# Three buffers in place of two for the tile of delta, in the preparation between the scan loops

## The chip, the cores and the metric

The kernel runs on one core of one Trainium2 chip. The metric is the device time of one execution in microseconds (us); lower is better. It is given as the median of several runs. One execution was also taken by the hardware profiler, and the profile and its trace come from that one.

## What is computed

A stack of four layers works on images x of shape (4, 64, 64, 96). The first two are selective-scan layers (the change lies in them), the last two are an attention without softmax and a feed-forward net. A scan layer, cut to what matters here:

```python
xz = einsum('bhwc,ec->bhwe', groupnorm(x), in_proj_w)      # E = 192, then z beside it
xc = silu(depthwise_conv3x3(xx) + conv_b)
xs = stack([x_hw, x_wh, x_hw[..., ::-1], x_wh[..., ::-1]]) # four directions, L = 4096 steps each
x_dbl = einsum('bkdl,kcd->bkcl', xs, x_proj_weight)        # dts (6), B (16), C (16)
delta = softplus(einsum('bkrl,kdr->bkdl', dts, dt_projs_weight) + dt_projs_bias)
# scan: h = exp(delta * A) * h + delta * B * u ;  y = sum_n h * C
y = layernorm(y_0 + flip(y_2) + back(y_1) + back(flip(y_3))) * silu(z)
out = x + einsum('bhwe,ce->bhwc', y, out_proj_w)
```

What the scan needs of each direction is delta itself and the product of delta and u. Delta has to reach the scan in nearly full precision, although it passes through a bf16 matmul there; so it is cut into three bf16 parts that add up to it.

## The kernel before

The batch is worked in two pairs of images, and with two scan layers that makes four phases. Each phase has a preparation, a scan loop, and a finish. `run` (L699) goes through the phases: it builds the preparation of phase p side by side with the finish of phase p-1, then the scan loop of phase p. So on the time axis a scan loop is followed by a gap in which the next preparation and the last finish share the engines, and then by the next scan loop. Before the first loop there is a preparation alone. After the last loop come a finish alone and the two token layers. The text calls the stretches between the scan loops, and the one before the first, "gaps".

Inside a scan loop the order of instructions on every engine is written out by hand (`manual_schedule`, L490). In the gaps it is not: there a scheduler orders each engine's instructions at build time, from the dependencies, the buffers and its own estimate of times. Each engine then takes its instructions strictly in that order at run time, and waits at the first one that is not ready. The DMAs are issued by the SP engine, from its own queue of instructions, also in order.

A preparation (`prepare`, L151) reads x, takes the statistics of the group norm, and runs `convolve` (L231) for each of the two images: a matmul (L251), the copy of its result into a padded tile (L254), nine taps of the convolution on VectorE (L268; the first, L266, on ScalarE), silu (L271), and a scaled copy that is stored for the finish (L276, L282). The second image's convolution runs between the calls of `steps` for the first image.

`steps` (L284) is where the change lies. There are 32 calls in a preparation: two images, eight chunks of 512 steps, two of the four directions; each call also does the opposite direction, so it makes a pair of tiles. In order:

- the matmul to dts, B and C (L291), and two copies into `xd`, forward and mirrored (L294, L295);
- the store of B and C (L303), and for both directions the matmul to delta's argument, into a PSUM tile `d` with two buffers (L308);
- then, for each of the two directions, a tile `dl` of delta (96 x 2 x 512 float32): softplus on ScalarE (L316); the first bf16 part, a cast on ScalarE (L317); the product with u on VectorE (L318); delta less its first part, written over delta on VectorE (L319); two stores of the product (L321); the second part, a cast on GpSimd (L322); the third part on VectorE (L323); the store of the three parts (L324).

`dl`, `parts`, `du_sb` and `xd` come from the pool `steps`, made with two buffers for each name (L168). A tile that is asked for when all its buffers are in use has to wait until the last reader of the oldest is done. For `dl` that is L323. For `parts` and `du_sb` it is the landing of their stores.

The finish (`finish`, L546) loads the scan's results (`yk`, L581, and `ud_f`, L571), adds the four directions through matmuls (L594, L603, copied out by L610), normalises (L633 to L648), multiplies with silu of z (L660, L663, L667), transposes (L674, L681) and projects (L685, L687), and stores the new x (L693).

Of the kernel before, what the change touches and what calls it, by code (L numbers as in the profile page):

```python
# [9 lines left out]
F32 = mybir.dt.float32  # L10
# [12 lines left out]
C = 96  # L23
# [6 lines left out]
TC = 512  # L30
# [25 lines left out]
def scan_view(t, k, c):  # L56


    part, half = t.ap[0], t.ap[1]
    if k == 0:  # L60
        off, steps = TC * c, (HW, 1)
    elif k == 1:
        off, steps = ROWS * c, (1, HW)
    elif k == 2:
        off, steps = L - 1 - TC * c, (-HW, -1)
    else:
        off, steps = L - 1 - ROWS * c, (-1, -HW)
    return bass.AP(t.tensor, t.offset + off, [part, half, [steps[0], ROWS], [steps[1], HW]])


def view(t, off, *dims):

    return bass.AP(t.tensor, t.offset + off, [t.ap[0]] + [list(d) for d in dims])


def rows(t):

    if len(t.shape) == 2:
        return t.rearrange("p (r w) -> p r w", w=HW)
    return t.rearrange("p h (r w) -> p h r w", w=HW)  # L80
# [50 lines left out]
class Scans:  # L131
# [152 lines left out]
    def steps(self, ph, sp, xc, xp, dt_w, i, k, c):  # L284


        nc, cst = self.nc, self.cst
        u = scan_view(xc, k, c)
        ps = self.bank()
        for h in range(2):  # L290
            nc.tensor.matmul(rows(ps[:XD2]), xp[:, k, h], u[:, h], start=h == 0, stop=h == 1)  # L291
        xd = sp.tile([XD2, TC], F32, name="xd")

        nc.scalar.activation(xd[:XD], ps[:XD], AF.Identity, bias=cst.one_row[:XD])  # L294
        nc.scalar.activation(  # L295
            xd[64:], view(ps[64:XD2], TC - 1, (-1, TC)), AF.Identity, bias=cst.one_row[64:]
        )
        yield
        both = []
        for back in range(2):  # L300
            at = 64 * back
            g, cc = 2 * (k + 2 * back) + i, NC - 1 - c if back else c
            nc.sync.dma_start(ph.bc[cc][:, g], xd[at : at + 2 * NS])  # L303
            both.append((g, cc, scan_view(xc, k + 2 * back, cc), self.p_d.tile([C, 2, TC], F32, name="d")))
        for m in range(2):
            for back, (_, _, _, ps) in enumerate(both):
                part = slice(64 * back + 2 * NS, 64 * back + XD)
                nc.tensor.matmul(  # L308
                    ps[:, m], dt_w[part, k, m * C : (m + 1) * C], xd[part], start=True, stop=True
                )  # L310
        yield
        for g, cc, u, ps in both:
            delta = sp.tile([C, 2, TC], F32, name="dl")
            parts = sp.tile([C, NP16, 2, TC], BF16, name="parts")
            du = sp.tile([C, 2, TC], F32, name="du_sb")
            nc.scalar.activation(delta, ps, AF.Softplus)  # L316
            nc.scalar.copy(parts[:, 0], delta)  # L317
            nc.vector.tensor_tensor(rows(du), rows(delta), u, ALU.mult)  # L318
            nc.vector.tensor_tensor(delta, delta, parts[:, 0], ALU.subtract)  # L319
            for copy in range(2):  # L320
                nc.sync.dma_start(ph.du[cc][copy, g, :E].rearrange("(h e) t -> e h t", h=2), du)  # L321
            nc.gpsimd.tensor_copy(parts[:, 1], delta)  # L322
            nc.vector.tensor_tensor(parts[:, 2], delta, parts[:, 1], ALU.subtract)  # L323
            nc.sync.dma_start(  # L324
                ph.delta[cc][g].rearrange("n (h q) t -> q (n h) t", h=2),
                parts.rearrange("q n h t -> q (n h) t"),
            )
            yield
# [660 lines left out]
```

## Time and profile before

| | |
|---|---|
| median of 3 runs | 11985.35 us (11978.79 to 12007.12) |
| the profiled execution's own time | 11973.68 us |
| its span in the trace | 11971.9 us |
| granted TensorE clock, mean over the span | 0.826 of full |
| busy: TensorE matmul | 8659.6 us (72%) |
| busy: VectorE | 10052.3 us (84%) |
| busy: ScalarE | 7321.2 us (61%) |
| busy: GpSimd | 7465.3 us (62%) |

Times are in us, lengths of one instruction in nanoseconds where a row says "mean ns". PE is TensorE, PEld its weight load, DVE VectorE, ACT ScalarE, POOL GpSimd, and SP the engine whose queue issues the DMAs. In the page each engine has a row of 40 slices of the span; a digit is the busy share of a slice in tenths, and PEclk is the clock that TensorE was granted, in tenths of full speed. A row of the timeline gives start, length, engine, line, operation, and what is written and read; in brackets stands how long the engine was idle before it and what ended the wait. A row of waits gives who waited for what, the total, how often, and the longest.

### The profile page before, as it was taken

The page shows a single profiled execution, that of the slowest core. Times are in us where ns is not written, and L with a number is a line of the kernel's source. Part 1 is how long each engine was busy: PE and PEld are TensorE (multiplying, and loading weights), DVE is VectorE, ACT ScalarE, POOL GpSimd, SP SyncE. Part 2 cuts the span into 40 slices and gives each one's busy share as a digit, 9 for nine tenths or more (in the row PEclk, how much of TensorE's full clock was granted, in tenths as well). Part 3 has the DMA queues.
Part 4 walks back from the last instruction along what each step waited for, and adds up shares of the span by engine and source line. Part 5 has one row for each costly group of instructions (what it writes and reads, how often), then busy time and mean ns, then how long its engine had stood idle before and what let it go on. Part 6 is the DMA issues. An engine that isn't in the chain of part 4 may idle for free.

```text
span 11971.9 us, 337755 instructions
## 1 busy us (share of the span) xinstructions
PE 8659.6 (72%) x144960; PEld 4597.6 (38%) x144960; DVE 10052.3 (84%) x10351; ACT 7321.2 (61%) x12109; POOL 7465.3 (62%) x2316
## 2 busy tenths in 40 slices
PE   3567777765767777765777777766677777777777
PEld 1124444442334444442334444433234444444333
DVE  6679999987769999987769999986769999993667
ACT  4556666655556666655556666654557666662556
POOL 0169999960149999970149999970139999990000
PEclk8579999986679989886679999986668999998887
DMA  3677777764677777765677777764677777763110
GB/s 98 185 244 254 255 252 252 252 206 138 197 231 255 254 256 257 257 216 143 193 226 256 258 257 252 258 219 136 199 221 258 255 254 250 254 232 125 18 21 11
DMA packets 952267, 2501.23 MB, mean 209 GB/s; under 512 B 324494, under 2 KB 607220, under 8 KB 819316
## 3 DMA queue, kind: packets, MB, share of 16 engines
q1 hardware_dynamic: 950772, 2479.63, 62.8%
q8 instruction: 1142, 18.71, 0.7%
q14 instruction: 353, 2.89, 0.1%
HBM read 1965.42 MB, written 513.80 MB: 207 GB/s over the span
## 4 chain that ended last, share of the span: by engine, by line
DMA 56%; PE 12%; DVE 11%; SPq 10%; ACT 5%; issue 4%; POOL 2%; POOLq 0%; DVEq 0%; ACTq 0%
DMA h<-du 52%; SPq L399 9%; DVE xc L268 4%; PE f L594 2%; POOL parts L322 2%; PE d L308 1%; PE c L291 1%; DVE parts L323 1%; DVE dl L319 1%; DVE du_sb L318 1%; DMA yk<-y 1%; PE c L251 1%; PE f L603 1%; PE f L674 1%; PE f L660 1%
## 5 line engine op out<-in xcount | busy, mean ns | idle before, releaser
L409 POOL TENSOR_TENSOR h<-h,b 128x1536 f32<-128x1536 f32 x2048 | 7021.1, 3461 | 533.5 <-DMA h<-du 191.9
L426 DVE TENSOR_TENSOR_SCAN h<-a,carry,h 128x512 f32<-128x512 f32 x5376 | 6345.7, 1259 | 174.6 <-POOL h L409 171.9
L419 ACT ACTIVATE a<-a,a_col 128x512 f32<-128x512 f32 x6144 | 4031.0, 664 | 1856.7 <-PE a L415 1830.9
L444 PEld LDWEIGHTS y<-h,cw 128*32 128x32 f32 x131072 | 2786.7, 128 | 3501.2 <-issue 1310.9
L444 PE MATMUL y<-h,cw 128*32 128x48 f32 x131072 | 3660.1, 266 | 527.3 <-DVE h L426 211.6
L415 PE MATMUL a<-dlt,rep 72*128 72x512 bf16 x6144 | 2526.8, 422 | 1302.3 <-DVE h L426 1212.9
L322 POOL CAST parts<-dl 96x1024 bf16<-96x1024 f32 x256 | 416.1, 1630 | 2793.0 <-DVE dl L319 2587.0
L456 ACT COPY d<-y 128x384 f32<-128x384 f32 x2048 | 979.8, 478 | 475.0 <-PE y L444 429.8
L426 DVE TENSOR_TENSOR_SCAN h<-a,h 128x512 f32<-128x512 f32 x768 | 868.3, 1200 | 165.5 <-ACT a L419 142.6
L415 PEld LDWEIGHTS <-rep 72*128 72x128 bf16 x6144 | 487.2, 98 | 829.0 <-issue 587.8
L308 PE MATMUL d<-xd,dt_w 7*96 7x512 f32 x1024 | 631.7, 905 | 237.5 <-ACT dl L316 149.6
L268 DVE SCALAR_TENSOR_TENSOR xc<-xp,conv_w,xc 96x512 f32<-96x512 f32 x1024 | 713.8, 756 | 54.8 <-ACT xc L266 38.9
L826 POOL MEMSET tn<- 1x4096 f32 x8 | 27.8, 3507 | 862.3 <-PE pa L846 515.1
L316 ACT ACTIVATE dl<-d 96x1024 f32<-96x1024 f32 x256 | 258.4, 1018 | 449.5 <-DVE parts L323 429.1
L318 DVE TENSOR_TENSOR du_sb<-dl,xc 96x1024 f32<-96x1024 f32 x256 | 416.2, 1633 | 116.7 <-ACT dl L316 73.0
L291 PE MATMUL c<-xc,x_proj 96*103 96x512 f32 x512 | 452.3, 1024 | 82.1 <-ACT xc L271 42.7
L594 PE MATMUL f<-yk,perm 128*128 128x384 f32 x1024 | 429.6, 564 | 95.4 <-DMA yk<-y 72.8
L251 PE MATMUL c<-rawi,in_w 96*96 96x512 f32 x256 | 206.0, 915 | 397.0 <-DVE rawi L247 312.1
L319 DVE TENSOR_TENSOR dl<-dl,parts 96x1024 f32<-96x1024 f32 x256 | 309.6, 1217 | 210.8 <-ACT parts L317 209.3
L323 DVE TENSOR_TENSOR parts<-dl,parts 96x1024 bf16<-96x1024 f32 x256 | 329.1, 1292 | 160.4 <-POOL parts L322 158.0
L308 PEld LDWEIGHTS d<-xd,dt_w 7*96 7x96 f32 x1024 | 171.8, 222 | 642.9 <-ACT dl L316 229.7
L361 ACT ACTIVATE cw<-c,gmask 128x256 f32<-128x256 f32 x512 | 286.0, 570 | 116.4 <-DMA dlt<-delta 58.1
(116 smaller groups left out, 5802.0 us busy)
## 6 DMA issues: line engine op xcount, KB each, us to landing
h<-du SPq DMA_DIRECT2D x1024, 768.0 KB
h<-du SPq DMA_DIRECT2D x2048, 384.0 KB
du<-du_sb SPq DMA_DIRECT2D x512, 384.0 KB
delta<-parts SPq DMA_DIRECT2D x256, 576.0 KB
dlt<-delta SPq DMA_DIRECT2D x512, 288.0 KB
y<-d SPq DMA_DIRECT2D x2048, 48.0 KB
yk<-y SPq DMA_DIRECT2D x256, 384.0 KB
ud<-xu SPq DMA_DIRECT2D x128, 192.0 KB
```

The costliest lines, as they stand in the source:

```text
L268: nc.vector.scalar_tensor_tensor(rows(acc), src, w, rows(acc), ALU.mult, ALU.add)
L291: nc.tensor.matmul(rows(ps[:XD2]), xp[:, k, h], u[:, h], start=h == 0, stop=h == 1)
L308: nc.tensor.matmul(ps[:, m], dt_w[part, k, m * C : (m + 1) * C], xd[part], start=True, stop=True)
L322: nc.gpsimd.tensor_copy(parts[:, 1], delta)
L399: self.nc.sync.dma_start(u.h[32 * first : 32 * (first + quarters), e : e + n].rearrange("p e t -> p (e t)"), source.rearrange("a g e t -> ...
L409: self.nc.gpsimd.tensor_tensor(h, h, b, ALU.mult)
L415: self.nc.tensor.matmul(u.a[n], self.cst.rep[:, h], u.dl[:, e], start=True, stop=True)
L419: self.nc.scalar.activation(u.a[n], u.a[n], AF.Exp, scale=u.ph.a_col[:, at : at + 1])
L426: self.nc.vector.tensor_tensor_scan(u.h[:, n], u.a.pop(n), u.h[:, n], 0.0 if u.c == 0 else u.ph.carry[:, at : at + 1], ALU.mult, ALU.add,)
L444: self.nc.tensor.matmul(view(u.y[32 * j : 32 * j + 32], l2 * EB, (8 * EB, 4), (1, EB)), u.ph.cw[u.c][:, l1, 8 * j + l2], view(u.h, 64 * l1 ...
L456: self.nc.scalar.copy(u.d[:, :, :, l1], u.y[:, : 32 * EB].rearrange("p (t h x) -> p t h x", t=4, h=2))
L594: nc.tensor.matmul(ps[:, : 4 * C].rearrange("p (w v e) -> p w v e", w=4, v=nv), cst.perm[:, k], view(t, off, (sw if k < 2 else -sw, 4), (1 ...
```

## The change

The tile of delta in `steps` gets three buffers of its own. The other tiles of the pool keep two. The operations are the same; the order on the engines is again the scheduler's.

```diff
         for g, cc, u, ps in both:
-            delta = sp.tile([C, 2, TC], F32, name="dl")
+            delta = sp.tile([C, 2, TC], F32, name="dl", bufs=3)
             parts = sp.tile([C, NP16, 2, TC], BF16, name="parts")
             du = sp.tile([C, 2, TC], F32, name="du_sb")
             nc.scalar.activation(delta, ps, AF.Softplus)
```

## The prediction

> **What bounds the kernel now.** I read the page first: the slices, then the chain that ended last. In the slices the 99999 stretches of DVE are the four scan loops; between them lie the stretches that the change touches. The chain's largest part, 52%, is the scan loops' load h<-du, which the change doesn't reach.
>
> ```profile
> span 11971.9 us, 337755 instructions
> DVE  6679999987769999987769999986769999993667
> PEclk8579999986679989886679999986668999998887
> ```
>
> By the first and last scan (L426) in the trace the loops run from 701 to 2599, 3437 to 5322, 6161 to 8035 and 8898 to 10769 us, so the gaps before them last 701, 838, 839 and 863 us. The first holds a preparation alone, the other three a preparation beside the finish of the phase before.
>
> Second, the windows of two kinds of gap (us, then busy time and count of PE, PEld, DVE, ACT, POOL, then clock and DMA). The reader is to see that in the first gap's end no engine but PE is near full, and that PE runs at half its clock; in a later gap's end PE is the fullest too.
>
> ```profile
> 550.00:600.00 50.00, 43.33 (x48) 11.27 (x47) 31.31 (x24) 21.01 (x24) 12.25 (x8) 0.50 0.77 224
> 3150.00:3250.00 100.00, 86.29 (x220) 39.88 (x220) 59.43 (x86) 52.58 (x64) 14.19 (x11) 0.67 0.73 214
> ```
>
> Third, the timeline of one pair of tiles in the first gap's end (A and B: the two directions of one call of steps; start, length).
>
> ```profile
> 544.43 1.22 DVE L323 TENSOR_TENSOR parts<-dl,parts 96x1024 bf16<-96x1024 f32 x1 [0.94 <-POOL parts L322]
> ...
> 545.75 1.02 ACT L316 ACTIVATE dl<-d 96x1024 f32<-96x1024 f32 x1 [5.32 <-DVE parts L323]
> ...
> 546.67 1.03 ACT L317 CAST parts<-dl 96x1024 bf16<-96x1024 f32 x1
> ...
> 547.73 1.22 DVE L319 TENSOR_TENSOR dl<-dl,parts 96x1024 f32<-96x1024 f32 x1 [2.08 <-ACT parts L317]
> ...
> 549.07 1.04 POOL L322 CAST parts<-dl 96x1024 bf16<-96x1024 f32 x1 [4.68 <-DVE dl L319]
> ...
> 550.14 1.22 DVE L323 TENSOR_TENSOR parts<-dl,parts 96x1024 bf16<-96x1024 f32 x1 [1.19 <-POOL parts L322]
> ...
> 551.29 1.22 DVE L318 TENSOR_TENSOR du_sb<-dl,xc 96x1024 f32<-96x1024 f32 x1
> ...
> 551.46 1.02 ACT L316 ACTIVATE dl<-d 96x1024 f32<-96x1024 f32 x1 [2.47 <-DVE parts L323]
> ...
> 552.50 1.04 ACT L317 CAST parts<-dl 96x1024 bf16<-96x1024 f32 x1
> ...
> 553.58 1.22 DVE L319 TENSOR_TENSOR dl<-dl,parts 96x1024 f32<-96x1024 f32 x1 [1.08 <-ACT parts L317]
> ...
> 556.87 1.22 DVE L323 TENSOR_TENSOR parts<-dl,parts 96x1024 bf16<-96x1024 f32 x1 [0.93 <-POOL parts L322]
> ```
>
> ACT takes its instructions in their order, and that order has the softplus L316 of a later tile ahead of the cast L317 of the tile before it. So L317, which needs nothing of L316, stands behind its wait for a free delta buffer: L323 ends, L316, L317, L319, L322, L323, one ring for every tile. A pair takes 12.44 us here; where u is read with the other stride L318 takes 1.9 us and the pair 13.1. The mean is 12.78, over 14 pairs from 513 to 692 us.
>
> Fourth, what ACT waited for in a later gap, 2790 to 3440 us (total, times, longest).
>
> ```profile
> ACT dl L316 <- DVE parts L323: 97.3, 28, 6.8
> ...
> ACT dl L316 <- PE d L308: 3.4, 3, 1.3
> ```
>
> **The change part by part.** *Removed:* the wait of L316 for L323 of the tile two before; it becomes one for the tile three before. *Moved:* the built order puts, on ACT, A' and B' of L316 together ahead of L317 of B (before: A' alone, and B' ahead of L317 of A'). On PE the four L308 of a pair interleave (A, B, A, B in place of A, A, B, B). In the first gap's end the order of DVE and SP is the same in both, POOL's everywhere; so no DMA passes another there. In the later gaps DVE and SP shift by a place or two. *Added:* one table load ahead of L271 in each later gap (67 for 66), and 4096 bytes per partition. The scan loops have the same order and addresses.
>
> *First gap's end.* B' of L316 now waits for L323 of A, and L317 of B still stands behind it. From the end of L323 of A to the end of L323 of B it stays 5.71 us (550.14+1.22 less 544.43+1.22). The other half is freed: L317 of A' stands behind the two xd copies only and is done early, so after L323 of B DVE goes straight on: L318 to 1.15, L319 to 2.29, POOL's cast from 2.41 for 1.92 (L318 of B' lies beside it, as at 554.92), L323 to 5.58. Sum 5.71+5.58 = 11.29 for 12.44, a gain of 1.15. With the long L318 (1.9) and cast (2.60) the same adding gives 12.67 for 13.12: 0.45. Mean 0.80, times 14 pairs: **11 us**.
>
> What comes next there, and what is late: L317 of A' needs the parts of A written out. Its DMA is issued 0.06 us after L323; at 691.68 one was issued whose buffer L317 took at 695.63, 3.95 later. So L317 can start 4.0 us after L323 of A, and is needed at 5.7: covered by 1.7 us. PE: eight L308 passes of 0.93 and four of L291 (3.74) are 11.18 us a pair at half clock, under the new 11.98 by 0.8. That is also the far end: with the ring gone altogether PE bounds the gain at 1.60 a pair, 22 us.
>
> *First gap before 513.* DVE has the convolution's taps to do; few steps of the chain there lie on L316's wait. I take 2 us, from 0 to 5.
>
> *Later gaps.* The same pattern fills their last 290 us (16 pairs), but at 17.9 us a pair (287 us from 3150 to 3437), since finishing work runs between. ACT waited there 69.0+11.9 us for L323, in 22 waits. If each were on the path as in the first gap (29 waits for 11 us), a gap would gain 8.5. Followed along the chain, 6 of these waits lie on it, against 28 in the first gap's end: 2.4. I take 4, nearer the chain's value, since PE is over 86% busy: 12 us for three gaps (0 to 26).
>
> *Table loads.* Row: ACT_TABLE_LOAD 1283 ns, and the activation starts 0.02 us after it (2837.82+1.28, next at 2839.12). The Trainium skill (ScalarE: Activation LUTs, What ACT_TABLE_LOAD costs) speaks harder against the change: a switch costs the load plus a drain, 2.66 us. By the row three cost 3.8 us, by the rule 8.0; the trace shows no such drain, so the row holds. ACT is 53% busy there and half of it is hidden: 2 us.
>
> A second rule reads this as a bigger gain: gaps that repeat on an engine can mean too little memory for the next tile (Perfetto Trace Analysis, Optimization Strategy). DVE's work of a pair is 2 x (1.57+1.22+1.22) = 8.0 us; if its gaps closed, PE's 11.18 would be the pace and the end would gain 22. But the row of L319 names L317 as what ended the gap, and half of those waits keep their place in ACT's order; so 11.
>
> *Sum:* -11 -2 -12 +2 = **-23 us**. The profiled execution took 11973.68 (span 11971.9), 11.7 under the median of the runs; so 11950.7 for it, and 11962 on the median of 11985.35. The far ends of the terms give -53 and, with nothing gained in the later gaps and 8.0 for the loads, -3.
>
> **The rivals.**
>
> *A much larger gain.* DVE waited for L317 53.5 us in a later gap's preparation and 47.9 in the first gap's second half. If these waits set the pace everywhere and half of them go, it is (3 x 53.5 + 47.9)/2 = 104 us: 11881. For it: ACT stands still 117 us per later gap for L323. Against it: the chain passes through only 6 of these waits there.
>
> *PE takes the wait's place; slower.* With two L316 ahead of it, L317 of B now also stands behind PE's second tile: B' of d is complete after all eight passes, 7.44 us, where A' was complete after four, 3.72. In the first gap PE is early enough. In the later gaps PE also does L594, L603 and L660 between, and L317, yt and z all queue behind the waiting L316. It decides where d of B' comes later than L323 of A; today L316 waits for PE 3.4 us a gap against 97.3 for DVE, so PE is ahead, but by one tile less from now on. If in 11 pairs (the 200 us from 3150 on, at 17.9 each) it is 2 us late, three gaps lose 66; with the first gap's gain and 0 elsewhere, +53: 12038.
>
> *It does nothing:* parts and du keep two buffers. If their landing came as late as L323 does, the pace would stay: 11985. The 1.7 us of slack speaks against it.
>
> **How the numbers follow.** My forecast has 0.62, and its own range is 11932 to 11982; the larger gain 0.16, PE's wait 0.15, nothing 0.07. About 0.3%, 36 us, is what a measurement of this kernel can tell from no change (its three runs lie 28 us apart). Below 11949 lies the larger gain with 0.14 and 0.10 of the forecast: faster 0.24. Above 12021: PE's wait, 0.14. The rest, 0.62, is within. The range runs from 11915, which takes in part of the larger gain, to 12010.
>
> **What would show it.** Right: L316 waits for L323 once a pair, not twice, in the first gap's end, the pair there takes near 12.0 us, and the first gap ends about 13 us earlier. L319's wait of 1.08 or 0.38 is gone and the 2.08 stays. Wrong: L316 <- PE d grows to tens of us in a later gap (the slower rival); L317 <- DMA delta appears in each pair (nothing gained); a scan loop's length changes by over 5 us; or a later gap shortens by over 15.

## The result and the profile after

The median of seven runs is 11953.92 us (11927.42 to 11962.63) after the change and 11985.35 us (11978.79 to 12012.14) before it. The ratio is 0.9965, with a 95% interval of 0.9951 to 0.9978: a gain, on the edge of the 0.3% (36 us) that the prediction set as measurable. The medians lie 31 us apart, the means 42. The forecast was 11962.

The page of the kernel after: span, one of the slice rows, and two rows of the costliest groups (busy us, mean ns, then idle time before them and what ended most of it).

```profile
span 11960.8 us, 337751 instructions
...
DVE  6779999977779999987769999986769999993667
...
L308 PE MATMUL d<-xd,dt_w 7*96 7x512 f32 x1024 | 532.4, 894 | 298.7 <-ACT dl L316 150.8
...
L316 ACT ACTIVATE dl<-d 96x1024 f32<-96x1024 f32 x256 | 258.0, 1019 | 322.7 <-DVE parts L323 260.2
```

The slices of VectorE have hardly moved. The two groups have: before, L316 stood idle for 449.5 us, 429.1 of them for L323, and L308 was busy for 631.7 us. The two profiled spans differ by only 11.1 us. Measured to the first real scan, the four gaps are 46.9 us shorter in sum (3357.3 to 3310.4), but the four scan loops took 36.1 us more in this execution (7411.5 to 7447.6). That part is not the change: another build of the two-buffer kernel (c_two below) took 7444.5 us in its loops, and another of the three-buffer kernel (c_three) 7438.9. The loops of one build thus differ from execution to execution by as much as the change is worth, one pair of spans says little, and the text compares gaps.

A gap is measured below from its start (the start of the program, or the end of the last scan before it) to the start of its last L323, the last work of its preparation. This avoids a slip of the prediction: the gap ends that it gave were the first record of L426, which lies up to 37 us ahead of the first scan.

| | first gap | second | third | fourth |
|---|---|---|---|---|
| before | 701.2 | 833.3 | 827.8 | 834.7 |
| after | 688.7 | 825.3 | 820.4 | 819.8 |

The timeline of the kernel after, one pair in the first gap's end (start, length, engine, line; in brackets the idle time before it and what ended that).

```profile
543.13 4.43 PE L308 MATMUL d<-xd,dt_w 7*96 7x512 f32 x8 [4.78 <-ACT xd L294]
...
544.88 1.04 ACT L317 CAST parts<-dl 96x1024 bf16<-96x1024 f32 x1 [1.09 <-DMA delta<-parts]
544.94 1.22 DVE L323 TENSOR_TENSOR parts<-dl,parts 96x1024 bf16<-96x1024 f32 x1 [1.19 <-POOL parts L322]
...
546.08 1.22 DVE L318 TENSOR_TENSOR du_sb<-dl,xc 96x1024 f32<-96x1024 f32 x1
...
547.40 1.22 DVE L319 TENSOR_TENSOR dl<-dl,parts 96x1024 f32<-96x1024 f32 x1
...
548.54 1.22 DVE L318 TENSOR_TENSOR du_sb<-dl,xc 96x1024 f32<-96x1024 f32 x1
...
550.70 1.22 DVE L323 TENSOR_TENSOR parts<-dl,parts 96x1024 bf16<-96x1024 f32 x1 [0.94 <-POOL parts L322]
551.98 0.30 SPq L324 DMA_DIRECT2D delta<-parts  x1
552.01 1.02 ACT L316 ACTIVATE dl<-d 96x1024 f32<-96x1024 f32 x1 [4.10 <-DVE parts L323]
...
552.93 1.03 ACT L317 CAST parts<-dl 96x1024 bf16<-96x1024 f32 x1
...
553.99 1.22 DVE L319 TENSOR_TENSOR dl<-dl,parts 96x1024 f32<-96x1024 f32 x1 [2.08 <-ACT parts L317]
...
556.88 1.04 ACT L317 CAST parts<-dl 96x1024 bf16<-96x1024 f32 x1 [1.63 <-DMA delta<-parts]
```

One half of the ring is left: L316 at 552.01 waits for the L323 of 550.70, the cast L317 stands behind it, and L319 waits 2.08 us for the cast. In the other half the cast (544.88) is over before DVE has done L318, and L319 starts without a wait for it.

The waits of ACT in the first gap's end, 505 to 692 us, in the kernel before (total, times, longest).

```profile
ACT dl L316 <- DVE parts L323: 107.2, 29, 5.5
ACT parts L317 <- DMA delta<-parts: 5.2, 1, 5.2
```

The same in the kernel after.

```profile
ACT dl L316 <- DVE parts L323: 64.0, 14, 5.5
ACT parts L317 <- DMA delta<-parts: 29.5, 17, 4.2
...
```

L316 now waits for L323 once a pair, not twice. The second row is the landing of the parts' store, one wait before and 17 after: a new wait, the next thing to be late. A pair now takes 11.47 us (544.94 to 556.41), and 12.87 us where u is read with the other stride; before it took 12.44 and 13.12.

A window of the kernel after (us, then busy time and count of PE, PEld, DVE, ACT, POOL, then clock and DMA).

```profile
550.00:600.00 50.00, 33.63 (x50) 10.48 (x48) 32.04 (x25) 21.14 (x24) 13.87 (x9) 0.50 0.82 238
```

In the first gap's end PE is busy for 33.63 of 50 us where it was 43.33, at the same clock of 0.50 and with more matmuls (50 for 48).

The waits of ACT in the second gap of the kernel after (2771 to 3421 us).

```profile
ACT dl L316 <- DVE parts L323: 57.7, 14, 6.6
...
ACT dl L316 <- PE d L308: 10.8, 7, 3.1
```

The wait for L323 fell from 97.3 us; the one for PE, which carried the slower rival, grew from 3.4 to 10.8.

### The profile page after: what moved, and what is told of

Same layout as the page of the kernel before. It is cut to its first block, busy times and chain, and to the rows that moved or that the text cites. A ratio compares the mean times of both kernels' runs of the same rounds, so it can differ in the third digit from the quotient of the medians.

```text
span 11960.8 us, 337751 instructions
## 1 busy us (share of the span) xinstructions
PE 8551.3 (71%) x144960; PEld 4578.9 (38%) x144960; DVE 10052.2 (84%) x10351; ACT 7336.3 (61%) x12112; POOL 7480.3 (63%) x2316
## 5 line engine op out<-in xcount | busy, mean ns | idle before, releaser
L426 DVE TENSOR_TENSOR_SCAN h<-a,carry,h 128x512 f32<-128x512 f32 x5376 | 6352.4, 1259 | 202.1 <-POOL h L409 198.5
L426 DVE TENSOR_TENSOR_SCAN h<-a,h 128x512 f32<-128x512 f32 x768 | 867.9, 1200 | 174.6 <-ACT a L419 149.5
L308 PE MATMUL d<-xd,dt_w 7*96 7x512 f32 x1024 | 532.4, 894 | 298.7 <-ACT dl L316 150.8
L291 PE MATMUL c<-xc,x_proj 96*103 96x512 f32 x512 | 443.4, 1006 | 81.8 <-ACT xc L271 41.9
L318 DVE TENSOR_TENSOR du_sb<-dl,xc 96x1024 f32<-96x1024 f32 x256 | 414.1, 1624 | 97.7 <-ACT dl L316 48.8
L323 DVE TENSOR_TENSOR parts<-dl,parts 96x1024 bf16<-96x1024 f32 x256 | 329.1, 1293 | 174.4 <-POOL parts L322 173.2
L316 ACT ACTIVATE dl<-d 96x1024 f32<-96x1024 f32 x256 | 258.0, 1019 | 322.7 <-DVE parts L323 260.2
L319 DVE TENSOR_TENSOR dl<-dl,parts 96x1024 f32<-96x1024 f32 x256 | 309.4, 1216 | 162.1 <-ACT parts L317 159.6
L308 PEld LDWEIGHTS d<-xd,dt_w 7*96 7x96 f32 x1024 | 161.6, 219 | 607.4 <-ACT xd L294 211.6
```

The lines of the kernel that those rows point to most:

```text
L308: nc.tensor.matmul(ps[:, m], dt_w[part, k, m * C : (m + 1) * C], xd[part], start=True, stop=True)
L426: self.nc.vector.tensor_tensor_scan(u.h[:, n], u.a.pop(n), u.h[:, n], 0.0 if u.c == 0 else u.ph.carry[:, at : at + 1], ALU.mult, ALU.add,)
```

## The experiments

Theory: in the gaps ACT's queue is in order, and L316 at its head holds up the cast L317 behind it; a third buffer frees half of these waits. Rivals: the gain comes from somewhere else in the gaps (the order that the scheduler finds for other engines, the stores), or from the scan loops.

All twelve runs, each against runs of the kernel before on the same chip. The later gaps are means over three of them.

| run | dl buffers | other | ratio (95%) | first gap | later gaps |
|---|---|---|---|---|---|
| c_two | 2 | | 1.0004 (0.9996 to 1.0012) | 698.3 | 827.5 |
| c_three | 3 | | 0.9949 (0.9933 to 0.9965) | 686.1 | 817.2 |
| e_first | 3, first gap only | | 0.9987 (0.9980 to 0.9994) | 689.3 | 833.3 |
| e_later | 3, later gaps only | | 0.9960 (0.9946 to 0.9974) | 697.5 | 814.9 |
| e_order2 | 2 | order forced | 0.9994 (0.9986 to 1.0001) | 674.8 | 836.5 |
| e_order3 | 3 | order forced | 0.9982 (0.9975 to 0.9990) | 672.4 | 835.9 |
| e_four | 4 | | 0.9930 (0.9915 to 0.9944) | 681.9 | 808.7 |
| e_parts3 | 2 | parts has 3 | 0.9962 (0.9947 to 0.9976) | 679.0 | 820.2 |
| e_order_first | 2 | order forced in the first gap | 0.9988 (0.9979 to 0.9997) | 672.3 | 828.7 |
| e_four_order | 4 | order forced in the first gap | 0.9902 (0.9888 to 0.9915) | 668.3 | 808.1 |
| e_sum | 2 | one cast moved in each later gap | 1.0000 (0.9988 to 1.0011) | 701.4 | 827.0 |
| e_four_all | 4 | order forced | 0.9977 (0.9968 to 0.9987) | 671.8 | 828.9 |

**The two kernels again (c_two, c_three).** Each is built once more with no other edit than `bufs=2` or `bufs=3`.

> The kernel with two buffers once more, for a second trace of the same instructions. In the first pair of traces the four gaps of the changed kernel were together 67 us shorter (12.5, 8.6, 9.0, 36.3) and its scan loops 56 us longer, though the change leaves the scan loops' order and addresses alone. If the loops vary by themselves from execution to execution, this trace shows loops that differ from the first one's by 10 us or more, and a last gap near 838 in place of 863. If three buffers make the loops slower, the loops stay within 3 us of 1898, 1884, 1874 and 1871. Ratio 1.000 either way.

> The kernel with three buffers once more. Gaps within 2 us of 689, 829, 830 and 826 if the gaps are what the change sets; loops anywhere from 1870 to 1900 if they vary by themselves, near 1893 each if the change made them slower. Time 25 to 40 us under two buffers.

The two-buffer build came out as the kernel before, and the three-buffer build a little faster than the first measurement, with overlapping intervals (0.9951 to 0.9978 and 0.9933 to 0.9965). The gain is real and lies between 0.2 and 0.7%. The loops of c_two lie 33 us in sum from those of the first trace with the same instructions, so they vary by themselves, as c_two's expectation put it.

**In which gaps? (e_first, e_later)**

```diff
-            delta = sp.tile([C, 2, TC], F32, name="dl")
+            delta = sp.tile([C, 2, TC], F32, name="dl",
+                            bufs=3 if ph.pre == "L0_" and ph.pair == 0 else 2)
```

> Three buffers in the first gap alone, two in the later ones. If the first gap's ring is what gives, the first gap is 689 us as with the full change, the later ones 838, and the time falls by 12 to 13 us (ratio 0.9990). If the later gaps carry the gain, the time falls by under 5.

> Three buffers in the later gaps alone. By the forecast's terms they give 12 less 2 of table loads, 10 us in all; by the first pair of traces 8.8, 7.7 and 13.8 us up to the last L323, 30 us in all. If the waits of the later gaps lie mostly off the path, 10 or less; if they lie on it, 20 to 30 (ratio 0.9975 to 0.9983). The first gap stays 701.

(e_later has the condition turned round.) The first gap alone is worth 0.13% of 12011, 16 us (7 to 24 by the interval); the later gaps alone 0.40%, 48 us (31 to 65). That is more than either case of e_later's expectation, and the prediction had the weights the other way about: 13 for the first gap, and 12 less 2 for the later ones. The gaps of the traces say the same. First gap: 699.6 us mean over the four kernels with two buffers and the scheduler's own order there (before, c_two, e_later, e_sum), 688.0 over the three with three buffers (after, c_three, e_first): -11.6. Later gaps: 830.4 over four kernels with two (before, c_two, e_first, e_order_first), 818.0 over three with three (after, c_three, e_later): -12.4 each, -37 for the three.

**The order of the queue without the third buffer (e_order2, e_order3).** Each L316 is told to stand behind the L317 of the tile before it on ACT; dl keeps two buffers in e_order2 and has three in e_order3.

```diff
-            nc.scalar.activation(delta, ps, AF.Softplus)
-            nc.scalar.copy(parts[:, 0], delta)
+            with ExitStack() as behind:
+                if ph.cast is not None:
+                    behind.enter_context(self.tc.issue_after(ph.cast))
+                nc.scalar.activation(delta, ps, AF.Softplus)
+            ph.cast = nc.scalar.copy(parts[:, 0], delta).ins
```

> Two buffers as before, but the softplus L316 of each tile may be issued on ScalarE only after the cast L317 of the tile before it. The order of VectorE in the first gap's end stays as before. If what costs is the order on ScalarE (L317 stuck behind L316's wait), the ring is gone although the buffers are still two: L316 still waits for L323 of the tile two before, but L317 of the other tile is done by then, and a pair takes about 11.3 us, near TensorE's 11.2, for 12.78: 20 us in the first gap alone, and 30 to 60 us in all. If what costs is the number of buffers, a pair still takes 12.8 us and nothing is gained.

> Three buffers and the same order as in the run before this one. If the order is the cause, the third buffer adds little to it: within 10 us of two buffers with that order. If the buffers are the cause, it is as the changed kernel, 31 us under the kernel before, and the order adds nothing.

In the first gap the order with two buffers (674.8) gains twice what the third buffer does (688.0), and the third buffer on top adds only 2.4 us. So there the ring was made by ACT's order and not by the number of buffers: this is the theory's core, and it holds. In the later gaps the same order loses: 836.5 and 835.9 against 830.4 and 818.0. The loss comes late. At tile 32 of the 64, e_order2 is 5.3 us ahead of the two-buffer mean; by tile 52, beside the finish, it is 6.5 us behind. These two builds load ACT's table 70 times in a later gap where two buffers have 66; at 1283 ns that is at most 5 us of it. What else goes with the loss is told below (L308 on PE). So e_order2 as a whole gained nothing that can be told from noise (0.9994, up to 1.0001), where its expectation had 30 to 60 us.

**More buffers (e_four, e_parts3).** `bufs=4` for dl; or `bufs=3` for parts with dl at two.

> Four buffers for delta, the order on ScalarE in the first gap's end is that of three. The softplus that stands ahead of L317 then waits for a tile one further back, which is long done, so the last wait of the ring goes: L319's idle time of 2.08 us goes too, and a pair in the first gap's end takes 11.2 to 11.5 us (TensorE's pace) for 12.17 with three: 10 us more there. If the landing of the stores of parts is the next bound, a pair stays at 12 and L317 waits for the DMA in each pair. In all 10 to 40 us under three buffers, or the same in the second case.

> Two buffers for delta, three for parts. Here the scheduler itself puts each L317 right behind its own L316. If the order is the cause this is as good as the forced order with two buffers, a pair near 11.3 us, without any third delta buffer. If delta's buffers are the cause, nothing is gained; then L316 waits for L323 as before, twice a pair, about 107 us in the first gap's end.

Four buffers are better than three in every gap: 681.9 and 808.7. With three buffers for parts the scheduler puts each L317 behind its own L316 by itself, and the first gap falls to 679.0 with dl at two. Each of these builds changes buffers and order together, so neither alone tells which of the two gains. The waits of ACT in e_four in the first gap (495 to 670 us).

```profile
ACT parts L317 <- DMA delta<-parts: 83.5, 27, 6.5
...
```

A window of e_four there (columns as above).

```profile
550.00:600.00 50.00, 34.87 (x51) 10.77 (x49) 36.75 (x28) 24.21 (x28) 11.16 (x9) 0.50 0.88 256
```

The wait for L323 is gone. What ACT now waits for is the landing of the parts, 27 times, with the DMA engines 88% busy. PE, at 34.87 of 50 us, is not the bound in this build. Its pairs take 11.3 us, as the first case of the expectation had it, but not for the reason given there (TensorE's pace).

**The order in the first gap alone (e_order_first, e_four_order).** The condition of the edit above becomes `ph.cast is not None and ph.pre == "L0_" and ph.pair == 0`. The kernel of e_four_order has this condition, four buffers and the order in the first gap only, while its expectation speaks of the order in all gaps. The kernel which that text describes is e_four_all, below.

> Two buffers; each L316 is put behind the L317 of the tile before it, but only in the first gap; the later gaps are left to the scheduler. Theory (in the first gap the order on ScalarE makes the ring, and the forced order costs time only in the later gaps): the last L323 of the first gap at 673 to 677 us as with the order forced everywhere (699.8 without it), pairs of 11.0; the later gaps as with two buffers, 829 +-6; sum -25 us, ratio 0.998 +-0.001. Rival (in the first gap it is the number of buffers, and 675 came by a side effect): 690 or more, ratio 0.999 or more. Second rival (a later gap inherits the earlier start of its predecessor, and so loses again): the later gaps at 837 or more, ratio 1.000.

> Four dl buffers, and in all gaps each L316 put behind the L317 of the tile before it. Theory (the forced order gains in the first gap and loses in the finish's tail of each later gap, whatever the number of buffers): first gap 672 us +-4, later gaps 836 +-5 each in place of 809 with four buffers alone, so +10 -85: near 75 us over four buffers alone, ratio 0.999 +-0.001. Rival (the loss in the later gaps came of too few buffers behind the forced order): later gaps near 810, ratio 0.992 or less, the best of all.

With two buffers the first gap is 672.3 us, as with the order everywhere, and the later gaps (828.7) are those of two buffers: what the first gap gains is not lost again in the next. Four buffers with the order in the first gap keep the later gaps of e_four (808.1) and take the first to 668.3. At 0.9902, 11887.82 us median, this is the fastest of all the kernels here. The waits of ACT in e_order_first (495 to 675 us; its lines stand four later, so L321 is the cast and L327 the third part).

```profile
ACT parts L321 <- DMA delta<-parts: 88.5, 30, 5.2
ACT dl L320 <- DVE parts L327: 3.9, 6, 1.1
```

A window of e_order_first there.

```profile
540.00:590.00 50.00, 48.00 (x54) 12.87 (x54) 36.38 (x27) 22.68 (x27) 10.39 (x9) 0.50 0.88 254
```

The ring's wait has shrunk to 3.9 us with two buffers. PE is busy for 48 of 50 us and the parts' landing is waited for in each tile: here both are near their limits.

**Four buffers and the order everywhere (e_four_all).**

> Four dl buffers, and each L316 behind the L317 of the tile before it in all gaps. (The run e_four_order, whose expectation speaks of all gaps, has this order in the first gap alone.) Theory (the forced order loses in the finish's tail of each later gap, whatever the number of buffers): first gap 668 to 672 us as with the order in the first gap alone, later gaps 836 +-5 each in place of 808, ratio 0.998 +-0.001. Rival (the loss in the later gaps came of too few buffers behind the forced order): later gaps near 810, ratio 0.991 or less.

The later gaps are 828.9 us, 21 more than with the order in the first gap alone. The forced order costs time beside the finish whatever the number of buffers, as the theory had it; its 836 was 7 us too high, so the extra buffers still take off some of the loss.

**What gains in the later gaps (e_sum).** Seen tile by tile, about half of a later gap's gain comes at one place. Start of L323 of some tiles (counted from 0), from the start of the gap, means over the later gaps:

| tile | 8 | 12 | 32 | 48 | 63 |
|---|---|---|---|---|---|
| two buffers (4 kernels) | 314.1 | 360.9 | 544.9 | 689.4 | 830.4 |
| three (3 kernels) | 312.4 | 353.4 | 537.9 | 680.2 | 818.0 |
| four (e_four, e_four_order) | 313.6 | 354.6 | 539.4 | 676.4 | 808.4 |
| e_sum | 312.7 | 359.0 | 543.6 | 687.6 | 827.0 |

Between tiles 8 and 12 two buffers take 46.8 us (43 to 49 in single gaps) and three 41.0. The timeline of ACT and DVE before the change, at this place:

```profile
2926.03 0.48 ACT L610 COPY s<-f 128x384 f32<-128x384 f32 x1 [5.88 <-PE f L603]
2936.61 0.48 ACT L610 COPY s<-f 128x384 f32<-128x384 f32 x1 [10.09 <-PE f L603]
2936.98 1.04 ACT L317 CAST parts<-dl 96x1024 bf16<-96x1024 f32 x1
...
2938.06 1.22 DVE L319 TENSOR_TENSOR dl<-dl,parts 96x1024 f32<-96x1024 f32 x1 [6.49 <-ACT parts L317]
```

Two copies of the finish wait 16 us for PE, the cast stands behind them, and DVE's L319 then waited 6.49 us for the cast. The timeline of PE before the change:

```profile
2927.26 3.72 PE L308 MATMUL d<-xd,dt_w 7*96 7x512 f32 x4
...
2934.92 1.65 PE L603 MATMUL f<-unit,ud_f 96*128 96x96 f32 x8
```

The L603 that the second copy needs stands behind passes of L308. In the kernel after, the first of these two copies runs much earlier, beside the copy ahead of it. The timeline of ACT after the change:

```profile
2899.29 0.86 ACT L610 COPY s<-f 128x384 f32<-128x384 f32 x2
```

Neither of the copies in this row waits: PE has their L603 ahead of the passes L308. The timeline of PE after the change:

```profile
2897.98 1.03 PE L603 MATMUL f<-unit,ud_f 96*128 96x96 f32 x8
2898.94 1.96 PE L308 MATMUL d<-xd,dt_w 7*96 7x512 f32 x8
```

So I moved the cast alone: with two buffers, the 14th and 15th L610 of a finish stand behind the L317 of the 11th tile. On ACT one instruction changes its place in each later gap; POOL's and SP's order stays whole, DVE's but for one place in one gap, and PE's but for one pair of matmuls (L660) moved in each gap.

```diff
+                with ExitStack() as behind:
+                    if self.sums in (13, 14) and len(self.casts) > 10:
+                        behind.enter_context(self.tc.issue_after(self.casts[10]))
-                nc.scalar.copy(
+                    nc.scalar.copy(
...
+                self.sums += 1
```

> Two buffers; one ScalarE instruction moved in each later gap: the two copies L610 that waited for PE's L603 (5.9 and 10.1 us in the trace of before) stand behind the L317 of the eleventh tile, which stood behind them. Theory (with three buffers the later gaps gain because this L317, or what stands with it, no longer sits behind those copies): from the third part L323 of tile 8 to that of tile 12 about 43 us in place of 48.9, the later gaps near 824 in place of 829.7 each, sum -18, ratio 0.9985 +-0.001. Rival (the gain needs PE's own order, with L603 ahead of the passes L308, since the next L316 still stands behind the copies): 47 to 49 us, later gaps 827 to 833, ratio 1.000. The first gap is as with two buffers in both, near 700.

The rival came nearer. The timeline of ACT in e_sum (lines: L318 the cast, L614 the copies, L317 the softplus):

```profile
2923.14 1.04 ACT L318 CAST parts<-dl 96x1024 bf16<-96x1024 f32 x1 [0.51 <-DMA delta<-parts]
2927.17 0.48 ACT L614 COPY s<-f 128x384 f32<-128x384 f32 x1 [2.98 <-PE f L604]
2937.47 0.48 ACT L614 COPY s<-f 128x384 f32<-128x384 f32 x1 [9.82 <-PE f L604]
...
2939.26 1.02 ACT L317 ACTIVATE dl<-d 96x1024 f32<-96x1024 f32 x1
```

Counted from the L323 of tile 8 in its own trace, the cast runs 16 us earlier (5.8 us after it, for 22.1), but the next softplus, which still stands behind the copies, only 2.4 us earlier (22.0 for 24.4). Tiles 8 to 12 take 46.3 us, and the ratio is 1.0000 (0.9988 to 1.0011): moving the cast gains little or nothing. By this the softplus, and with it PE's L603, has to move too. That is argued from the two traces and from e_sum's failure; no run moved L603 by itself. The third buffer is not needed at this place: e_order2, with two, takes 41.0, 43.6 and 40.9 us there.

**A rival for the later gaps that no run tests.** PE itself has less to do with the third buffer. The 256 passes of L308 in a later gap take less time where A and B alternate, and PE is the fullest engine there. Means of a later gap, from its start to its last L323, from all traces (us):

| kernels | length | L308 busy | PE busy |
|---|---|---|---|
| four buffers (e_four, e_four_order) | 808 | 122 | 526 |
| three (3 kernels) | 818 | 129 | 532 |
| three for parts (e_parts3) | 820 | 137 | 533 |
| two (4 kernels) | 830 | 148 | 557 |
| four, order forced (e_four_all) | 829 | 160 | 573 |
| two or three, order forced (e_order2, e_order3) | 836 | 167 | 582 |

The granted clock is 0.64 to 0.68 in all of them. The gaps follow PE's work, also where the forced order loses. So the third buffer may gain here because the order that came with it makes L308 20 us shorter, and the forced order may lose because it makes L308 19 us longer. The traces show only that the two go together, and e_four_all, with more work of PE than two buffers and no longer gap, shows that it is not all. No run changed the order of L308's passes alone, so the cause of the later gaps' gain stays open between this and the place of L603.

## Why the prediction was right or wrong

- **The ring (right).** Its signs came in: 14 waits for L323 for 29, pairs of 11.47 and 12.87 us in turn (12.17 in the mean) for 12.44 and 13.12 (12.78), the first gap 12.5 us shorter, L319's waits for L317 down from 28 to 16 with the 2.08 us kind left. The order forced with two buffers, which removes the wait, is the test of the cause.
- **The first gap, -13 (measured -11.6).** A pair gained near 0.61 us, not 0.80. The missing part is seen in the timeline: with the cast no longer late, L319 follows L318, whose operand it overwrites, and it starts 0.10 us after that ends (546.08+1.22, then 547.40), while the next L318, which doesn't depend on it, starts 0.08 us before L319 ends. That is 0.18 us a pair. In the means of the traces, 7.6 us of the gap's gain came from tile 36 on (about 528 us), for an estimate of 11, and 4.0 before, for an estimate of 2: the sum of the two terms is nearer than either of them.
- **PE's floor of 11.18 us a pair (wrong).** It added eight passes of L308 at 0.93 us. Where they are ordered A, B, A, B they take 4.43 us (543.13; L291 follows at 547.49), not 7.44, so the floor is 4.43+3.74 = 8.2 us. For A, A, B, B it holds: the forced order runs with PE at 48 of 50 us and pairs of 11.2 to 11.3 us. It changed no number of the forecast. The far end of -22 for the first gap's end was not reached by any kernel here; the largest gain, e_four_order's 31 us in the first gap, has 18 us from tile 36 on and 13 us before it, where the prediction allowed 5.
- **The later gaps, -12 (measured -37).** This is the term that was mis-sized. The prediction looked only at the last 290 us of a gap, and counted there which waits for L323 lay on the chain. In that stretch (tile 32 to the end) three buffers gain 5.4 us where it took 4: sized nearly right. The other 7.0 us of a gap lie before it, 5.8 of them at tiles 8 to 12, where the order that the scheduler found puts the finish's L603 and the cast at other places. The prediction had compared that order and named only a place or two and a table load. It had also named the interleaving of L308's passes and put it at nothing: L308 takes 129 us in a later gap for 148. Whether that is the cause is open, as told above.
- **The table loads, +2.** Not isolated. One more in each later gap cannot be more than 3.8 us, and the gaps gained all the same.
- **The bubbles' rule, 22 us for the first gap.** The bubbles did close to about that size: 25 us with two buffers and another order. So a shortage of memory was not what they needed; the row of L319, which names the cast, was the better guide to the cause, but the rule was the better guide to what could be gained there.
- **The slower rival.** Its wait, L316 for PE, reached 10.8 us in a later gap (15.1 in the next), not the tens that it needed, and PE's interleaved passes are ready sooner than it assumed.
- **Three signs that misled.** The wait of L317 for the parts' landing did appear in each pair, and yet the gain was there: the cast at 556.88 ends while DVE is at L318. And the sum of the scan loops changed by 36 us, which builds with the same number of buffers also do. By the prediction's own gap ends the last gap shortened by 36 us (862.6 to 826.3), which was to show it wrong; by the last L323 it is 14.9 us, just under the 15 that it set.

On the sum, -23 was forecast, and the gaps of the two traces give -43 (12.5+8.0+7.4+14.9); over all kernels it is -49. That the measured median lies only 8 us from the forecast is in part luck: the first comparison gave 31 us, the smallest of the values here, and c_three gave 62. The mechanism was right for the first gap; for the later gaps, which carry three quarters of the gain, the forecast was a third of it or less.

## What to carry to other kernels

Where an engine takes its queue in order and an instruction waits for a buffer, look at what stands behind it in its engine's queue: if an independent instruction is stuck there, its place in the queue may be worth more than the buffer, as here in the first gap (25 us for the order, 12 for the buffer). Where a scheduler orders the engines, a buffer also changes the order elsewhere, and with it the work of an engine that never touches the tile; compare the traces tile by tile over the whole stretch, and not only where the wait is longest. A forced order that helps alone can hurt beside other work, so it is put where it was shown to help: the order in the first gap and four buffers everywhere gave 0.9902.

## What was not expected of the hardware

- Two series of matmuls that read 7 partitions each, one from partition 32 and one from 96 of the same tile (L308), took less time together when their passes alternated: 4.43 us for eight at half clock, against 3.72 us for four in a row of one kind. This agrees with the Trainium skill (TensorEngine Tiling (Array Packing), Tiling Modes, Key Properties), by which small tiles on different partitions can load weights and multiply in parallel. Over the whole kernel L308's busy time fell by 99 us.
- With the DMA engines 82% busy, a store of the parts issued at 551.98 freed its buffer for the cast at 556.88, 4.9 us later; the prediction took 3.95. At 88% (e_four) ACT waited for this landing for 83.5 us in the first gap's end.
